# Gate terms on GpSimd, images' sum on VectorE, first gate at the head of the spectral part

## The chip, the cores and the metric

The kernel runs on one NeuronCore of a Trainium2 chip. The metric is the device time of one execution in microseconds; the time before is the median of three runs. The engines are called PE (TensorE), DVE (VectorE), ACT (ScalarE), POOL (GpSimd) and SP (SyncE, which here only issues DMAs).

## The reference

Two layers over x of shape 8x128x128x128 (images, channels, rows, columns), all in float32. Only the first layer is touched by the change. It computes, for each image:

```python
feat = gelu(batchnorm(conv2d(x, conv_w, padding=3, dilation=3)))      # 64 channels
F2 = fft2(feat)
attn = complex_softmax(einsum(l2norm(F2), conj(l2norm(F2))) * tau)    # within heads of 8 channels
out_f = abs(ifft2(attn @ F2))                                         # the mixture
cg = sigmoid(conv1x1(gelu(batchnorm(conv1x1(F2.real)))))              # the gate: 64 -> 4 -> 64
gate = abs(ifft2(cg * F2))                                            # the gated images
x = concatenate([out_f, gate], axis=1) + x
```

The second layer is a 3x3 convolution, a selective scan over eight tokens of every pixel, and a group norm, and takes the larger part of the time.

## The kernel before

`network` runs `layer0` and then `layer1`, with the result of the first in device memory (`x1`). `layer0` makes four passes over two images each; the two images' 64 channels fill the 128 partitions. A pass is `convolve` (the convolution, its transposes and the Gram matrix, 32 steps of four rows) and then `spectral`.

`spectral` works on groups of four channels of one image: 16 groups per image, n = 0 to 31 (`NP = 32`). The order of all engines' work is the order in which the program is written (`manual_schedule`): there is no planner, and every engine takes its own instructions strictly in that order. In iteration n of the loop (L444) stand, in this order:

- `columns(n)` (L288): the column transform on PE, into the PSUM banks `er` and `ei`.
- `gate_begin(n + 2)` (L310): the gate's base, four ACT instructions of 128x65 from the hidden map `hid`.
- `gated(n)` (L329): four DVE products of `er` or `ei` (PSUM) with the gate `cg` (SBUF), into `gp`.
- `rows(n + 1)` (L280): the row transform on PE, copied by ACT to `fa`.
- `rows_back(n - 1)` (L348): the last inverse transform on PE into `ops`; ACT takes the absolute value (L354), POOL adds the input images `xg` (L355), SP stores (L356).
- `gate_end(n + 2)` (L319): the gate's three remaining terms. Each is a product (L323) into the scratch tile `cgt` and an addition (L326) to `cg`, 128x260 elements; then ACT's sigmoid (L327), with a table load if ACT last used another set.
- `mixture()` (L377): from n = 3 on, once in an odd iteration and twice in an even one, four rows of the attention's output: PE into `pf` (one buffer of two banks), ACT's squares (L385, L386), DVE's sum (L387). For n of 1 and 2 the steps of `softmax` stand here instead.
- `columns_back(n)` (L340): PE into `zps`, and DVE's copy to `z` (L346).
- `roots()` (L394): after every fourth mixture, ACT's square root over 128x2048 (L397, with its own table load), POOL's addition of the input (L398, 128x2048), SP's stores and the loads for the next. Eight times in a pass.
- `load_gate(n + 3)` (L359): SP loads `xg`, into the buffer that the sum of group n releases in the next iteration.

After n = 24 there are no mixtures left. Every PSUM tile of `spectral` has one buffer: `ps`, `er`, `ei`, `zps`, `ops` and `pf` (two banks), beside `gram`. In SBUF `cg` and `xg` have three buffers, `cgt`, `fa`, `z`, `og` and `sq` two, `gp` one.

Ahead of the loop (L431 to L443) stand the hidden map of each of the two images (`rows` and `columns` of `mT`, then four Gelu instructions each), the first step of `softmax`, `rows(0)`, and both steps of the gate for groups 0 and 1.

The heart of what the change touches:

```python
for m in range(1, MID):
    t = f2.tile([P, 4, NF], F32, name="cgt")
    nc.vector.tensor_mul(t, hid[...].broadcast_to([P, 4, NF]), w2r[...].broadcast_to([P, 4, NF]))
    nc.vector.tensor_add(cgs[n], cgs[n], t)
nc.scalar.activation(cgs[n], cgs[n], AF.Sigmoid)
```

Of the kernel before, what the change touches and what calls it, by code (L numbers as in the profile page):

```python
# [10 lines left out]
AF = mybir.ActivationFunctionType  # L11
# [130 lines left out]
def layer0(ctx, tc, x, w0, c0, x1):  # L142
# [9 lines left out]
    nc = tc.nc  # L152
# [9 lines left out]
    def cf(name):  # L162
        at, n = C0[name]
        return ct[:, at:at + n]
# [32 lines left out]
    fT = big.tile([P, H, P], F32, name="fT")  # L197
# [68 lines left out]
    def spectral(p):  # L266

        with tc.tile_pool(name="l0_f1", bufs=1) as f1, \
# [9 lines left out]
            fas, cgs, zs, xgs, mix = {}, {}, {}, {}, {}  # L278

            def rows(key, src, j0):  # L280

                ps = p1.tile([P, 4, P], F32, name="ps")
                for k in range(4):
                    nc.tensor.matmul(ps[:, k], src[:, :, j0 + k], cf("fwd"), start=True, stop=True)
                fas[key] = f2.tile([P, 4, P], F32, name="fa")
                nc.scalar.copy(fas[key], ps)

            def columns(key, which):  # L288

                a, out = fas.pop(key), []  # L290
                for name, of_re, of_im in (("er", "cos", "sin"), ("ei", "nsin", "cos"))[:which]:
                    e = p1.tile([P, 4, NF], F32, name=name)
                    nc.tensor.matmul(
                        e, cf(of_re), a[:, :, 0:NF], start=True, stop=False, skip_group_check=True)
                    nc.tensor.matmul(
                        e[:, :, mid], cf(of_im), a[:, :, NF:P], start=False, stop=True,
                        skip_group_check=True)
                    out.append(e)
                return out

            def hidden(b):
                er, = columns(("m", b), 1)
                for m in range(MID):
                    nc.scalar.activation(
                        hid[:, b, m, :], er[:, m, :], AF.Gelu, bias=gt[:, m:m + 1], scale=gs[:, m:m + 1])

            def place(n):
                return n * 4 // CD, n * 4 % CD

            def gate_begin(n):  # L310
                b, c = place(n)
                cgs[n] = f3.tile([P, 4, NF], F32, name="cg")
                for i in range(4):
                    k = (c + i) * MID
                    nc.scalar.activation(
                        cgs[n][:, i, :], hid[:, b, 0, :], AF.Identity, bias=b2[:, c + i:c + i + 1],
                        scale=w2[:, k:k + 1])

            def gate_end(n):  # L319
                b, c = place(n)  # L320
                for m in range(1, MID):
                    t = f2.tile([P, 4, NF], F32, name="cgt")
                    nc.vector.tensor_mul(  # L323
                        t, hid[:, b, m:m + 1, :].broadcast_to([P, 4, NF]),
                        w2r[:, c:c + 4, m:m + 1].broadcast_to([P, 4, NF]))
                    nc.vector.tensor_add(cgs[n], cgs[n], t)  # L326
                nc.scalar.activation(cgs[n], cgs[n], AF.Sigmoid)  # L327

            def gated(n, e):  # L329
# [18 lines left out]
            def rows_back(n):  # L348
                (b, c), z = place(n), zs.pop(n)
                ops = p1.tile([P, 4, W], F32, name="ops")  # L350
                for i in range(4):
                    nc.tensor.matmul(ops[:, i, :], z[:, i, :], cf("inv"), start=True, stop=True)
                og, xg = f2.tile([P, 4, W], F32, name="og"), xgs.pop(n)
                nc.scalar.activation(og, ops, AF.Abs)  # L354
                nc.gpsimd.tensor_add(og, og, xg)  # L355
                nc.sync.dma_start(  # L356
                    x1[2 * p + b][CD + c:CD + c + 4, :, :].rearrange("c h w -> h c w"), og)

# [10 lines left out]
            def load_mixture(r0):  # L369
                mix[r0] = f2.tile([P, CH, W], F32, name="xr")  # L370
                for b in range(2):
                    nc.sync.dma_start(
                        mix[r0][b * CD:(b + 1) * CD], x[2 * p + b, 0:CD, r0:r0 + CH, :])
# [31 lines left out]
            def softmax(k):  # L405
                if k == 0:
                    nc.vector.tensor_copy(gm, gram)
                    nc.vector.tensor_mul(dg, gm, cf("ident"))
                    nc.vector.tensor_reduce(rn, dg, AX.X, ALU.add)
                    nc.vector.tensor_scalar(rn, rn, float(HW), NRM_EPS, ALU.mult, ALU.add)  # L410
                    nc.scalar.activation(rn, rn, AF.Sqrt)
                    nc.vector.reciprocal(rn, rn)
                    nc.vector.tensor_scalar(gm, gm, rn, None, ALU.mult)
                elif k == 1:
                    t = p1.tile([P, 2, 4, W], F32, name="pf")
                    nc.tensor.transpose(t[:, 0, 0, :], gm, cf("ident"))
                    nc.vector.tensor_scalar(gm, t[:, 0, 0, :], rn, tau_hw, ALU.mult, ALU.mult)
                    nc.vector.tensor_mul(gm, gm, cf("mask"))
                    nc.vector.tensor_add(gm, gm, cf("nmask"))
                    nc.vector.tensor_reduce(mx, gm, AX.X, ALU.max)  # L420
                    nc.vector.tensor_scalar(gm, gm, mx, None, ALU.subtract)
                    nc.scalar.activation(gm, gm, AF.Exp)
                elif k == 2:
                    nc.vector.tensor_reduce(rn, gm, AX.X, ALU.add)
                    nc.vector.reciprocal(rn, rn)
                    nc.vector.tensor_scalar(gm, gm, rn, None, ALU.mult)
                    t = p1.tile([P, 2, 4, W], F32, name="pf")
                    nc.tensor.transpose(t[:, 0, 0, :], gm, cf("ident"))
                    nc.vector.tensor_copy(pT, t[:, 0, 0, :])
# [3 lines left out]
            rows(("m", 0), mT, 0)  # L433
            hidden(0)
            rows(("m", 1), mT, MID)
            softmax(0)
            hidden(1)
            rows(0, fT, 0)
            load_mixture(H - CH)
            load_mixture(H - 2 * CH)  # L440
            for n in range(2):
                gate_begin(n)
                gate_end(n)  # L443
            for n in range(NP + 1):  # L444
                if n < NP:
                    e = columns(n, 2)
                    if n + 2 < NP:
                        gate_begin(n + 2)
                    gp = gated(n, e)
                    if n + 1 < NP:  # L450
                        b, c = place(n + 1)
                        rows(n + 1, fT, b * CD + c)
                if n > 0:
                    rows_back(n - 1)
                if n == NP:
                    break
                if n + 2 < NP:
                    gate_end(n + 2)
                if n >= START:
                    mixture()  # L460
                elif n > 0:
                    softmax(n)
                columns_back(n, gp)
                if n >= START and n % 2 == 0:
                    mixture()
                roots()
                load_gate(n + 3)
                if n == NP - 5 and 2 * p + 2 < B:
                    first_load(p + 1)
# [5 lines left out]
    with tc.manual_schedule(engines={E.PE, E.Activation, E.DVE, E.Pool, E.SP}):  # L475
        first_load(0)
        for p in range(B // 2):
            convolve(p)
            spectral(p)
# [593 lines left out]
```

## Time and profile before

| What | Value |
|---|---|
| Median of three runs | 15525.09 us (15520.91 to 15526.82) |
| The profiled execution: its time, its span | 15543.48 us, 15541.7 us |
| Granted clock of PE, mean | 0.98 |
| PE busy | 14740.9 us, 95% |
| DVE busy | 12858.9 us, 83% |
| POOL busy | 12025.9 us, 77% |
| ACT busy | 8249.8 us, 53% |
| POOL's sum of the images (L355), 128 times | 175.3 us, 1370 ns each |
| First layer ends in the profile at | about 2673 us |
| A pass's gate loop, from the first to the last z copy (first pass) | 358.4 to 675.8 us |

The page divides the span in 40 equal slices and gives the busy share of each engine in tenths. Its groups are instructions of one line, engine and shape: busy time and mean duration, then the engine's idle time before them and what ended most of it. The timeline gives start, duration, engine, line, and in brackets how long the engine was idle before and what released it. A table by stages gives each engine's busy time with the number of its instructions, the granted clock, the DMA share and the traffic.

### The profile page before, as it was taken

What the parts mean: (1) busy time and instruction counts of PE and PEld (TensorE: products, weight loads), DVE (VectorE), ACT (ScalarE), POOL (GpSimd) and SP (SyncE); (2) the same over time, 40 slices, a digit from 0 to 9 for tenths busy, and PEclk for the clock granted to TensorE, in tenths of its full rate; (3) what the DMA queues carried; (4) which work ended last, traced back from release to release, by engine and by line L of the source; (5) the groups of instructions that cost most, each with busy time, mean ns of one, the idle gap of its engine ahead of it and who ended that gap; (6) DMA issues with size and microseconds to landing.
All of it is one profiled execution on the core that took longest, in us unless ns stands there. A gap on an engine that the chain in (4) does not pass through costs nothing.

```text
span 15541.7 us, 200536 instructions
## 1 busy us (share of the span) xinstructions
PE 14740.9 (95%) x71816; PEld 5749.3 (37%) x71816; DVE 12858.9 (83%) x12667; ACT 8249.8 (53%) x9158; POOL 12025.9 (77%) x5796
## 2 busy tenths in 40 slices
PE   9899898999999999999999999999999999999996
PEld 4655556333333333333333333333333333333332
DVE  1423415999999999999999999999999999999995
ACT  1322314555555555555555555555555555555553
POOL 0101102899999999999999999999999999999996
PEclk9999999999999999999999999999999999999996
DMA  1323323666666666666666666666666666666665
GB/s 72 104 70 97 79 77 93 116 120 120 120 129 135 134 135 132 136 136 133 134 135 135 134 134 137 135 135 132 135 135 136 135 134 136 134 133 134 136 136 136
DMA packets 1075747, 1932.47 MB, mean 124 GB/s; under 512 B 123968, under 2 KB 255040, under 8 KB 1058368
## 3 DMA queue, kind: packets, MB, share of 16 engines
q1 hardware_dynamic: 1074176, 1917.29, 57.4%
q8 instruction: 571, 9.36, 0.2%
q14 instruction: 424, 3.47, 0.1%
q10 hardware_dynamic: 576, 2.35, 0.0%
HBM read 375.64 MB, written 201.33 MB: 37 GB/s over the span
## 4 chain that ended last, share of the span: by engine, by line
PE 58%; DVE 17%; issue 4%; ACT 3%; DMA 1%; POOL 0%; DVEq 0%; SPq 0%; POOLq 0%; ACTq 0%
PE da L693 18%; PE yps L759 8%; PE ups L693 7%; PE pm L134 7%; DVE da L724 6%; DVE h L732 4%; DVE h L708 4%; PE yps L765 4%; PE pm L645 3%; PE pm L778 3%; PE pm L657 3%; DVE hc L743 2%; PE da L638 2%; PE yps L749 2%; ACT da L698 2%
## 5 line engine op out<-in xcount | busy, mean ns | idle before, releaser
L738 POOL TENSOR_TENSOR hc<-h,cc 128x1024 f32<-128x1024 f32 x3584 | 8375.2, 2367 | 431.4 <-DVE h L732 409.1
L698 ACT ACTIVATE da<-da 128x1024 f32<-128x1024 f32 x3584 | 3618.7, 1010 | 4198.5 <-PE ups L693 2508.0
L708 DVE TENSOR_TENSOR h<-ups,bb 128x1024 f32<-128x1024 f32 x3584 | 4368.7, 1219 | 693.0 <-PE ups L693 313.5
L693 PE MATMUL da<-du,m_a 16*128 16x512 f32 x14336 | 4072.8, 644 | 139.3 <-DVE hc L743 135.2
L693 PE MATMUL ups<-du,m_u 16*128 16x512 f32 x14336 | 4119.2, 643 | 2.3 <-DVE h L708 1.3
L732 DVE TENSOR_TENSOR h<-da,h 128x1024 f32<-128x1024 f32 x2304 | 2821.2, 1224 | 79.1
L724 DVE TENSOR_TENSOR da<-da,h 128x1024 f32<-128x1024 f32 x2304 | 2820.1, 1224 | 6.9 <-ACT da L698 3.4
L134 PE MATMUL pm<-xin,l_wt 128*128 128x508 f32 (+1 forms) x4608 | 2413.0, 624 | 176.8 <-ACT xr L783 170.2
L730 POOL TENSOR_TENSOR h<-ah,h 128x1024 f32<-128x1024 f32 x768 | 1817.9, 2367 | 448.2 <-DVE ah L722 408.6
L693 PEld LDWEIGHTS da<-du,m_a 16*128 16x128 f32 x14336 | 1079.9, 184 | 2625.7 <-issue 1004.6
L759 PE MATMUL yps<-hc,l_ct 128*32 128x512 f32 x14336 | 1931.7, 611 | 0.0
L355 POOL TENSOR_TENSOR og<-og,xg 128x512 f32<-128x512 f32 x128 | 175.3, 1370 | 2126.3 <-ACT og L354 1065.7
L134 PEld LDWEIGHTS pm<-xin,l_wt 128*128 128x128 f32 x4608 | 751.7, 189 | 1620.6 <-issue 1390.6
L693 PEld LDWEIGHTS ups<-du,m_u 16*128 16x128 f32 x14336 | 1125.5, 184 | 379.4 <-DVE h L708 296.9
L241 DVE COPY fT<-tps 128x512 f32<-128x512 f32 x128 | 88.6, 692 | 1184.3 <-PE tps L240 1184.3
L698 ACT ACT_TABLE_LOAD x774 | 993.0, 1283 | 30.6 <-PE ups L693 1.7
L722 DVE TENSOR_TENSOR ah<-da,h 128x1024 f32<-128x1024 f32 x768 | 932.9, 1215 | 0.0
L134 PE MATMUL cps<-xin,l_wt 128*64 128x500 f32 (+1 forms) x4032 | 869.0, 584 | 0.0
L759 PEld LDWEIGHTS yps<-hc,l_ct 128*32 128x32 f32 x14336 | 283.8, 108 | 1376.7 <-issue 964.1
L652 POOL TENSOR_TENSOR u<-dt,xc 128x512 f32<-128x512 f32 x512 | 655.1, 1279 | 173.0 <-ACT dt L647 170.9
L235 ACT ACTIVATE feat<-cps,bn_t,bn_s 128x512 f32<-128x512 f32 x128 | 99.5, 777 | 1144.1 <-PE cps L134 1144.1
L647 ACT ACT_TABLE_LOAD x511 | 655.6, 1283 | 28.9 <-PE pm L645 1.1
(155 smaller groups left out, 15471.0 us busy)
## 6 DMA issues: line engine op xcount, KB each, us to landing
bb<-bc SPq DMA_DIRECT2D x2048, 256.0 KB
cc<-bc SPq DMA_DIRECT2D x2048, 256.0 KB
du<-dt SPq DMA_DIRECT2D x2048, 64.0 KB
du<-u SPq DMA_DIRECT2D x2048, 64.0 KB
xin<-x SPq DMA_DIRECT2D x112, 640.0 KB
xin<-x SPq DMA_DIRECT2D x48, 1408.0 KB
gn<-xr SPq DMA_DIRECT2D x256, 256.0 KB
v<-gn SPq DMA_DIRECT2D x256, 256.0 KB
```

The source lines that it names most:

```text
L134: nc.tensor.matmul(out[:, a:b, wa:wb], wt[:, t, :], src[:, r + dy + a - base:r + dy + b - base, wa + dx:wb + dx], start=(n == 0), stop=(n ...
L647: nc.scalar.activation(d["dt", hf], ps, AF.Softplus, bias=wf("dt_b"))
L652: nc.gpsimd.tensor_mul(d["u", hf], d["dt", hf], d["xc"][:, hf, :])
L693: nc.tensor.matmul(o, w, v, start=True, stop=True)
L698: nc.scalar.activation(da, da, AF.Exp)
L708: nc.vector.tensor_mul(h, d["ups", s], state_row(i, "bb", s // GP))
L722: nc.vector.tensor_mul(d["ah"], da, before)
L724: nc.vector.tensor_mul(da, da, before)
L730: nc.gpsimd.tensor_add(h, d["ah"], h)
L732: nc.vector.tensor_add(h, d["da", s], h)
L738: nc.gpsimd.tensor_mul(hc, d["h", s], state_row(i, "cc", t))
L759: nc.tensor.matmul(d["yps"][g * DI:(g + 1) * DI], gather[:, t % LP, :], d["hc", GP * t + g // GP][:, g % GP], start=False, stop=(t in (3, ...
```

## The change

Three edits, all in `spectral`:

1. `gate_end`: the three products and three additions are issued on GpSimd for n of 2 and up, and stay on VectorE for n of 0 and 1.
2. `rows_back`: ACT writes the absolute value back into PSUM (`ops`), and VectorE adds the input from there, in place of GpSimd.
3. The head: `gate_begin(0)` and `rows(0)` move ahead of `hidden(1)`, `gate_end(0)` ahead of `softmax(0)`; the loads of the mixtures and the gate of group 1 follow.

```diff
             def gate_end(n):
                 b, c = place(n)
+                eng = nc.vector if n < 2 else nc.gpsimd
                 for m in range(1, MID):
                     t = f2.tile([P, 4, NF], F32, name="cgt")
-                    nc.vector.tensor_mul(
+                    eng.tensor_mul(
                         t, hid[:, b, m:m + 1, :].broadcast_to([P, 4, NF]),
                         w2r[:, c:c + 4, m:m + 1].broadcast_to([P, 4, NF]))
-                    nc.vector.tensor_add(cgs[n], cgs[n], t)
+                    eng.tensor_add(cgs[n], cgs[n], t)
                 nc.scalar.activation(cgs[n], cgs[n], AF.Sigmoid)
...
                 og, xg = f2.tile([P, 4, W], F32, name="og"), xgs.pop(n)
-                nc.scalar.activation(og, ops, AF.Abs)
-                nc.gpsimd.tensor_add(og, og, xg)
+                nc.scalar.activation(ops, ops, AF.Abs)
+                nc.vector.tensor_add(og, ops, xg)
...
             rows(("m", 1), mT, MID)
+            gate_begin(0)
+            rows(0, fT, 0)
+            hidden(1)
+            gate_end(0)
             softmax(0)
-            hidden(1)
-            rows(0, fT, 0)
             load_mixture(H - CH)
             load_mixture(H - 2 * CH)
-            for n in range(2):
-                gate_begin(n)
-                gate_end(n)
+            gate_begin(1)
+            gate_end(1)
```

In the changed kernel two lines are added above these, so that L319 to L357 of before stand up to two lines later (the sigmoid at L329, the absolute value at L356, the sum at L357, POOL's large addition at L400).

## The prediction

> **What bounds the kernel now.** I read the page first: its slices of busy tenths say where the stages lie.
>
> ```profile
> span 15541.7 us, 200536 instructions
> ...
> DVE  1423415999999999999999999999999999999995
> ...
> POOL 0101102899999999999999999999999999999996
> ```
>
> A slice is 388.5 us. DVE and GpSimd are idle or light for some seven slices: that is the first layer, which ends at 2673 us in the timeline. The rest is the second layer, which the change doesn't touch. Within the first layer only the spectral part of each of the four passes changes. In the first pass it runs from 333 to 680 us, so four times about 345 us, 9% of the span, can move. The busy time by stage of that part:
>
> ```profile
> core 0: us, PE busy (x) PEld busy (x) DVE busy (x) ACT busy (x) POOL busy (x), PEclk, DMA share, GB/s
> 384.50:622.50 238.00, 192.53 (x927) 150.63 (x926) 144.75 (x252) 121.89 (x223) 59.67 (x27) 0.90 0.42 103
> 622.50:679.80 57.30, 53.07 (x331) 49.35 (x331) 38.21 (x79) 24.40 (x49) 16.17 (x10) 0.94 0.43 129
> ```
>
> While mixtures are interleaved (iterations 3 to 24, first row) PE is busy for 192.5 of 238 us; in the last iterations (second row) for 53.1 of 57.3. Near the end consecutive z copies stand at 659.02 and 665.09: 6.07 us per iteration, PE's own work. So the loop is PE's except where PE waits. The timeline shows where: after each of the eight `roots` of a pass. Iteration 9 of the first pass:
>
> ```profile
> 443.80 4.52 POOL L398 TENSOR_TENSOR feat<-feat,xr 128x2048 f32<-128x2048 f32 x1 [8.24 <-ACT feat L397]
> ...
> 445.08 3.53 DVE L326 TENSOR_TENSOR cg<-cg,cgt 128x260 f32<-128x260 f32 x1 [2.20 <-ACT cg L315]
> ...
> 448.28 1.46 POOL L355 TENSOR_TENSOR og<-og,xg 128x512 f32<-128x512 f32 x1
> ...
> 448.54 1.50 DVE L323 TENSOR_TENSOR cgt<-hid,l_wt 128x260 f32<-128x260 f32 x1
> ...
> 451.38 1.28 ACT L327 ACT_TABLE_LOAD   x1 [5.36 <-DVE cg L326]
> 452.67 0.42 ACT L327 ACTIVATE cg<-cg 128x260 f32<-128x260 f32 x1
> 453.00 0.58 ACT L385 ACTIVATE sq<-pf 128x512 f32<-128x512 f32 x1
> 453.61 0.58 ACT L386 ACTIVATE pf<-pf 128x512 f32<-128x512 f32 x1
> ...
> 454.22 0.69 DVE L387 TENSOR_TENSOR feat<-pf,sq 128x512 f32<-128x512 f32 x1 [2.92 <-ACT pf L386]
> 454.83 0.68 DVE L346 COPY z<-zps 128x512 f32<-128x512 f32 x1
> ...
> 455.66 2.05 PE L352 MATMUL ops<-l_ct,z 128*128 128x128 f32 x8 [5.25 <-ACT cg L315]
> ```
>
> Read it downwards. GpSimd's large add runs 443.80 to 448.32. The gate's add on DVE (0.43 us elsewhere) takes 3.53, the next product 1.50 (0.42 elsewhere) beside the images' sum. Then the sigmoid's table load, the sigmoid, the two squares queued behind it on ACT, their sum and the z copy on DVE, and at last PE, idle for 5.25 us and then at half clock (2.05 against 1.06). The gate's terms are what ends last there.
>
> **What the Trainium skill says.** "SBUF — State Buffer", Who interferes with whom: a VectorE instruction with two SBUF inputs blocks against a GpSimd one that reads SBUF; with one SBUF input, outside the 2-port modes, it doesn't. The trace agrees: 3.53 and 1.50 above, while the second layer's L708 (PSUM and SBUF) holds a mean of 1219 ns with GpSimd busy. "GPSIMD Engine Reference", Performance versus the Vector engine: about 2.6 cycles an element for two inputs, 4497 ns at 2048; the trace has 4.52 us. Same page, Performance pitfalls for Q7 kernels: reads with a step over 8 bytes cost about 50% more per element; no row here shows that. "ScalarE: Activation LUTs", What ACT_TABLE_LOAD costs: about 1283 ns; the trace has 1283.
>
> **Part 1: the gate's six terms (three products, three adds) go to GpSimd for n of 2 and up.** No row shows a 128x260 on GpSimd. Two rows of the page price it:
>
> ```profile
> L738 POOL TENSOR_TENSOR hc<-h,cc 128x1024 f32<-128x1024 f32 x3584 | 8375.2, 2367 | 431.4 <-DVE h L732 409.1
> ...
> L652 POOL TENSOR_TENSOR u<-dt,xc 128x512 f32<-128x512 f32 x512 | 655.1, 1279 | 173.0 <-ACT dt L647 170.9
> ```
>
> (2367-1279)/512 = 2.125 ns an element, 191 ns fixed, so 260 elements take 0.743 us (the line gives 4.54 at 2048; 4.52 is there). An add must wait for its product: I add 0.07, as from ACT's L354 end to GpSimd's L355 start in the first pass. A product needn't wait, and starts 0.04 before the last one's end (448.28 against 448.32). Six terms: 3x0.813 + 3x0.703 = 4.55 us; from the end of the gate's base on, 3.8, since the first product runs ahead.
> *Ordinary iterations.* In iteration 8 the base ends at 430.05, so the sigmoid starts at 433.9 against 434.34 now. The squares behind it wait for PE's mixture until 435.24 either way: nothing gained. ACT's loop, base 1.35 + 3.87 + sigmoid 0.33 = 5.55 us, stays under PE's 6.07.
> *Root iterations, seven per pass.* GpSimd now does the root's add and then all six terms, as the first product is queued behind the add too: 448.28 + 4.55 = 452.83, sigmoid at 452.90. The reload isn't late any more: in the built order of the changed program it waits only for ACT's own base and the sigmoid alone waits for GpSimd, whereas before the load waited for DVE. So 1.28 us of load is hidden, and the sigmoid comes at 452.90 against 452.67: +0.2 each, +1.4 per pass. The stall that the lock caused goes, and GpSimd's own queue takes its place.
> *The eighth root (n = 24)* has no squares behind it. There DVE's blocked terms hold the z copy until 640.22, PE stands 2.57 us and runs at half clock afterwards; the columns of n = 27 start at 646.30. After the change z is free at once; what is late next is ACT's fa copy, behind the sigmoid: GpSimd 637.3 + 4.55 = 641.9, sigmoid, base and fa to 644.2, and the columns then: -2.1, and half a step more without the half clock: -2.3 per pass.
>
> **Part 2: the images' sum goes to DVE, from PSUM.** `og<-ops,xg` has the form of L387, 0.69 us against 1.27 to 1.46 on GpSimd; ACT's L354 only changes where it writes, 0.60 as now. DVE gives up 6x0.43 and takes 0.69; with 61% busy in the first row above that is hidden. DVE now waits for og's store (ACT did), with the z copy queued behind it: before, this wait shows three times in all four passes, 3.4 us together, near a pass's end, and PE's work hid it: nothing. SP's loads wait for DVE in place of GpSimd, at the same places. The bank of `ops` is released by DVE and no longer by ACT, and the next pass's convolution waits for it (PE at 678.55, right after L354): +0.07 + 0.69, three times: +2.3 in all. No DVE instruction in the loop has two SBUF inputs any more outside softmax, so the lock has nothing to hold.
>
> **Part 3: the head.** Now the gated products start at 353.08. In the new order: base(0) at 339.99 to 341.43; its terms on DVE to 343.5; hidden(1) ends at 344.2 without its own reload (1.28 before); sigmoid(0) with load to 345.9; root load and rn to 347.4; base(1) to 348.9; its terms to 350.9; gated then: -2.2. Loads in the chain: three before, three after. In iteration 2 the softmax no longer follows the gate's terms on DVE (now 372.04): after L354 at 370.5 and the sum to 371.15 the three steps end at 371.95, PE at 372.05 against 372.88: -0.8.
>
> **Sum.** Per pass -2.2 - 0.8 + 1.4 - 2.3 = -3.9, four passes -15.6; + 2.3 at the seams; -0.6 for the last sum: -14 us. The profiled execution took 15543.48 us (span 15541.7 and 1.8 around), 18.4 over the median of 15525.09; I take the change from the median: 15511 us, -0.09%.
>
> **Bounds of the unknown price.** Below: nothing excludes a cheaper term; at -10% (0.67) the seven roots give 7x0.44 = 3.1 per pass more, and if the shorter idle of PE in the head (4.5 against 6.3 us) leaves the clock up, 1.6 more: -33 us, 15492. Above: the products read a weight that steps by 16 bytes; at +50% they take 1.11 and the mean term 0.93: roots 7x1.1 more, the ACT loop (rival a) at 6.5 against 6.07 in ten iterations 4.3, the mixtures' iterations some 4: 16, less 3.9: +12 per pass, 15575.
>
> **Rivals.** (a) *Slower: ACT's loop through GpSimd becomes the bound.* Every iteration passes base, terms, sigmoid on ACT in order. With terms of 1.0 us it takes 1.35 + 5.2 + 0.33 = 6.9, over 6.07; it decides from 0.84 on (5 terms fill 4.3). Ten iterations x 0.8, roots 7x1.7, mixtures some 8: +28, less 5 for the rest: +23 per pass, 15619. For it: an unmeasured broadcast form. Against it: L738 too has a broadcast operand and costs what the line says. (b) *Faster by more: the cheap end above,* 15492: the lock cost more than I see, in the ordinary iterations too (1.37 for the last add in many). Against it: PE or the root's queue ends last there. (c) *The load isn't hidden:* 1.28x7x4 = +36, 15547; against it stands the built order.
>
> **Chances.** Forecast with its neighbours, between 15494 and 15556: 0.63, with (c) in it at 0.05; (a) beyond that 0.20; (b) 0.17. A change under 0.2% (31 us) is about what a measurement of this kernel can't tell from none. The range takes the forecast's cases, most of (b) and the near half of (a): 15482 to 15575.
>
> **What would show it.** GpSimd 128x260 rows near 0.74 us; DVE's gate rows only for n of 0 and 1; no DVE row of 3.5; the sigmoid in root iterations 4.6 us after the root's add, its load long before; gated 2.2 us earlier in the head; the loop's last 6.07 unchanged. Terms over 0.84 us, or a load behind GpSimd's wait, would make me wrong.

## The result and the profile after

The changed kernel takes 15496.45 us (median of 20 runs, 15484.40 to 15508.01), the kernel before 15526.95 us (median of 20, 15520.91 to 15538.69): a ratio of 0.998, 95% interval 0.9973 to 0.9987. That is 30.5 us or 0.20% less, just at the border of what the prediction called no change; the interval lies wholly below 1. The forecast was 15511 us, 14 us less than before.

The page of the changed kernel, its span and the slices of VectorE and GpSimd:

```profile
span 15495.1 us, 200595 instructions
...
DVE  1211213999999999999999999999999999999995
...
POOL 0321304899999999999999999999999999999996
```

In the first layer's slices work has moved from VectorE to GpSimd; the rest reads as before. The table by stages of the first pass, over the same two stretches of the loop as before (from z copy 3 to z copy 23, and from there to the end of the pass):

```profile
379.80:612.30 232.50, 191.09 (x926) 149.90 (x926) 73.85 (x151) 122.15 (x224) 110.90 (x127) 0.90 0.42 105
612.30:667.60 55.30, 51.34 (x329) 47.52 (x329) 24.91 (x52) 25.12 (x51) 27.78 (x36) 0.99 0.45 138
```

VectorE's busy time in the first stretch falls from 144.8 to 73.9 us, GpSimd's rises from 59.7 to 110.9. The stretch itself gets only 5.5 us shorter, and PE's work and its granted clock (0.90) stay: 71 us of relief on an engine that had slack buy little.

The root iteration that the prediction took apart, in the timeline (start, duration, engine, line, work; in brackets the idle time before and what ended it):

```profile
439.23 4.52 POOL L400 TENSOR_TENSOR feat<-feat,xr 128x2048 f32<-128x2048 f32 x1 [9.76 <-ACT feat L399]
...
441.45 1.28 ACT L329 ACT_TABLE_LOAD   x1
...
443.71 0.63 POOL L325 TENSOR_TENSOR cgt<-hid,l_wt 128x260 f32<-128x260 f32 x1
444.41 0.74 POOL L328 TENSOR_TENSOR cg<-cg,cgt 128x260 f32<-128x260 f32 x1
...
447.21 0.73 POOL L328 TENSOR_TENSOR cg<-cg,cgt 128x260 f32<-128x260 f32 x1
...
447.98 0.42 ACT L329 ACTIVATE cg<-cg 128x260 f32<-128x260 f32 x1 [5.25 <-POOL cg L328]
...
450.14 0.68 DVE L348 COPY z<-zps 128x512 f32<-128x512 f32 x1
...
450.87 1.01 PE L354 MATMUL ops<-l_ct,z 128*128 128x128 f32 x3 [5.04 <-DVE z L348]
```

The table load now stands at 441.45, long before it is needed. The six terms follow GpSimd's large sum and take from 443.71 to 447.94. The sigmoid starts 8.75 us after that sum starts, where before it was 8.87 (452.67 - 443.80). PE idles 5.04 us instead of 5.25. So the stall is the same length, made of other parts.

GpSimd's new groups (busy time, mean ns of one, idle time before):

```profile
L328 POOL TENSOR_TENSOR cg<-cg,cgt 128x260 f32<-128x260 f32 x360 | 264.9, 736 | 357.1 <-issue 321.5 <-ACT cg L315 14.2
...
L325 POOL TENSOR_TENSOR cgt<-hid,l_wt 128x260 f32<-128x260 f32 x360 | 226.6, 630 | 1403.5 <-DVE cg L328 1403.5
```

The sum costs what the prediction's line gave (736 ns against 743), the product less (630 ns).

**Where the time went, per pass.** The z copies of the trace, one an iteration, give every part. The table has means of the four passes, before in us, the others as differences from it. Ordinary and root iterations are those between z copies 3 and 24: seven in which the sigmoid waits behind a square root, fourteen others. The seam runs from a pass's last z copy to the next pass's first Gelu (the fourth to the second layer's first matmul into `da`). The numbers in brackets are those of the experiments below. The median difference is each kernel's to the kernel before in the same comparison.

| Kernel | Convolution | Head | First three | Ordinary (14) | Roots (7) | Last seven | Seam | Sum x 4 | Median difference |
|---|---|---|---|---|---|---|---|---|---|
| before | 315.2 | 22.6 | 25.9 | 133.9 | 111.7 | 45.5 | 13.7 | | |
| after | +1.0 | -2.0 | -1.4 | -5.0 | -0.6 | -2.6 | +0.9 | -38.6 | -30.5 |
| terms alone (5) | 0.0 | +0.3 | +6.0 | +52.3 | +11.4 | +6.2 | -0.1 | +304.0 | +316.0 |
| sum alone (6) | 0.0 | -0.1 | +5.6 | +13.0 | -3.8 | -1.5 | +0.4 | +53.9 | +73.3 |
| head alone (3) | -0.1 | -2.3 | -0.2 | +0.6 | -0.1 | -0.6 | -0.1 | -10.8 | -10.1 |
| sum behind the terms (1) | 0.0 | -0.1 | -1.7 | -3.1 | -7.1 | -2.7 | +1.5 | -53.0 | -42.0 |
| after, bank by ACT (2) | 0.0 | -1.9 | -1.6 | -5.0 | -0.6 | -2.5 | -0.1 | -47.0 | -41.0 |
| after, products twice (4) | +1.0 | -1.8 | +2.3 | +7.1 | +14.0 | +1.9 | +0.2 | +99.2 | +102.6 |
| sum behind, head, old seam (7) | 0.0 | -2.4 | -1.2 | -3.0 | -7.4 | -2.7 | -0.3 | -67.7 | -51.9 |
| the same as 7, root's sum deferred (8) | 0.0 | -2.1 | -1.2 | -3.0 | -7.4 | -2.7 | -0.3 | -66.9 | -52.8 |
| the same as 7, early load (9) | -0.1 | -2.3 | -1.2 | -6.7 | -16.6 | -2.7 | -0.3 | -119.1 | -102.3 |
| after, root's sum deferred (10) | +1.0 | -2.1 | -1.2 | -2.8 | -25.8 | -3.8 | -0.3 | -139.7 | -133.0 |
| after, root's sum on VectorE (11) | 0.0 | -1.3 | -1.2 | -3.3 | -12.9 | -4.1 | -0.2 | -91.8 | -75.9 |
| last add on GpSimd (12) | 0.0 | -1.9 | -1.9 | -12.0 | -33.2 | -4.5 | -0.3 | -215.0 | -204.6 |

The profiled execution of before lay 16.5 us above its median (15543.48 against 15526.95). The sums over the passes come out up to 19 us lower than the differences of medians, and cells below about 0.6 say nothing: the head alone, which doesn't touch the ordinary iterations, shows +0.6 there.

### The profile page after: what moved, and what is told of

Read it like the earlier page. It is cut to its first block, busy times and chain, and to the rows that moved or that the text cites. A ratio compares the mean times of both kernels' runs of the same rounds, so it can differ in the third digit from the quotient of the medians.

```text
span 15495.1 us, 200595 instructions
## 1 busy us (share of the span) xinstructions
PE 14718.2 (95%) x71816; PEld 5738.3 (37%) x71816; DVE 12489.5 (81%) x12075; ACT 8246.5 (53%) x9158; POOL 12327.9 (80%) x6388
## 4 chain that ended last, share of the span: by engine, by line
PE 58%; DVE 17%; issue 4%; ACT 3%; DMA 1%; POOL 0%; DVEq 0%; SPq 0%; POOLq 0%; ACTq 0%
PE da L696 18%; PE yps L762 8%; PE ups L696 7%; PE pm L134 7%; DVE da L727 6%; DVE h L735 4%; DVE h L711 4%; PE yps L768 4%; PE pm L648 3%; PE pm L781 3%; PE pm L660 3%; DVE hc L746 2%; PE da L641 2%; PE yps L752 2%; ACT da L701 2%
## 5 line engine op out<-in xcount | busy, mean ns | idle before, releaser
L325 POOL TENSOR_TENSOR cgt<-hid,l_wt 128x260 f32<-128x260 f32 x360 | 226.6, 630 | 1403.5 <-DVE cg L328 1403.5
```

## The experiments

Line numbers in the profile lines are each kernel's own. No experiment leaves out part of the computation.

**1. The images' sum behind the terms** (e3_sum_late). My theory after seeing the result: in the ordinary iterations the lock on the gate's last term (VectorE's term is stretched from 0.43 to 1.38 us while GpSimd's sum of the images runs beside it) was on the path, and its end is the gain; GpSimd is not needed for it. The rival: the gain comes of VectorE being rid of the terms. The edit, to the kernel before:

```diff
-                nc.scalar.activation(og, ops, AF.Abs)
-                nc.gpsimd.tensor_add(og, og, xg)
+                nc.scalar.activation(ops, ops, AF.Abs)
+                return ops
...
                 if n + 2 < NP:
                     gate_end(n + 2)
+                if n > 0:
+                    images_sum(n - 1, ops)      # nc.vector.tensor_add(og, ops, xg), then the store
```

> The kernel before with one edit: the images' sum goes from GpSimd to VectorE and is issued after the next gate's terms instead of ahead of them; the terms stay on VectorE and the head stays as it was. In the kernel before, the images' sum on GpSimd runs beside VectorE's last term of the gate in ordinary iterations, and that term then takes 1.38 us where it takes 0.43 alone; so this edit takes that slowing away and nothing else that the change has. Theory 1 (the ordinary iterations' gain of some 5 us a pass came from this slowing of the last term, which held the sigmoid): the first-to-last distance of the images in a pass falls by 5 to 13 us, the last terms take 0.43 us, and the time is 15475 to 15505. Theory 2 (the gain came from VectorE being free of the terms themselves, so that its later work starts earlier): the time is 15518 or more, since VectorE then has 0.7 us more a group.

Measured: 15484.43 us, ratio 0.9973 (0.9962 to 0.9984). The first-to-last distance of the z copies falls by 14.7 us a pass, a little more than expected, and not where I had put it: 7.1 of it are in the seven root iterations. One of them in this kernel's timeline:

```profile
441.01 4.52 POOL L402 TENSOR_TENSOR feat<-feat,xr 128x2048 f32<-128x2048 f32 x1 [32.69 <-ACT feat L401]
...
442.30 3.51 DVE L326 TENSOR_TENSOR cg<-cg,cgt 128x260 f32<-128x260 f32 x1 [2.21 <-ACT cg L315]
...
446.99 0.43 DVE L326 TENSOR_TENSOR cg<-cg,cgt 128x260 f32<-128x260 f32 x1
...
447.50 1.28 ACT L327 ACT_TABLE_LOAD   x1 [4.28 <-DVE cg L326]
448.79 0.42 ACT L327 ACTIVATE cg<-cg 128x260 f32<-128x260 f32 x1
```

The block of 3.51 us by the root's sum stays, the second one (1.50 us in the kernel before) is gone: the sigmoid comes 7.78 us after the root's sum starts, 8.87 before. Without one instruction moved to GpSimd this kernel is as fast as the changed one or faster (the intervals of the two ratios overlap). So theory 1 holds in part: with the lock of the images' sum gone the ordinary iterations gain 3.1 us a pass, but more comes in the root iterations. The second theory, which asked for 15518 or more, falls. The edit moves the sum to VectorE as well as behind the terms; the new order alone, with the sum left on GpSimd, was not run. What the place is worth on VectorE, experiment 6 shows.

**2. The bank of the last group** (e6_seam). The changed kernel; in a pass's last group ACT writes to SBUF again:

```diff
-                nc.scalar.activation(ops, ops, AF.Abs)
-                nc.vector.tensor_add(og, ops, xg)
+                if n == NP - 1:
+                    nc.scalar.activation(og, ops, AF.Abs)
+                    nc.vector.tensor_add(og, og, xg)
+                else:
+                    nc.scalar.activation(ops, ops, AF.Abs)
+                    nc.vector.tensor_add(og, ops, xg)
```

> The changed kernel with one edit: for the last group of a pass alone, ScalarE writes its absolute value to SBUF as in the kernel before, and VectorE adds from there, so that the PSUM bank that the next pass's convolution needs is given back by ScalarE and not by VectorE. Theory A (the changed kernel's seam is longer because the bank waits for VectorE's sum, and the second half-speed stretch of TensorE after the seam follows from that longer idle time): the time from a pass's last image to the next pass's first Gelu falls from 11.0 to 10.0-10.3 us, the convolution after it from 316.1 to 314.8 us, together some 2 us in each of three seams, so 6 to 7 us: 15488 to 15491. Theory B (the half-speed stretch comes of the pass's shorter end or by chance): the seam shortens by 0.7 us and the stretch stays: 15494.

Measured: 15485.41 us, ratio to before 0.9974 (0.9965 to 0.9983). The three seams are 9.9 us long (after: 11.0) and the convolutions behind them 314.8 us (after: 316.1), 2.4 us a seam, 7 in all, as theory A asked; the time is 3 us under its band. (The intervals of the two kernels' ratios overlap; it is the trace that parts them.) The stages of 24 us from the start of the second pass's convolution, first of the changed kernel, then of this one (the last numbers but two are PE's granted clock):

```profile
666.00:690.00 24.00, 23.46 (x118) 10.03 (x120) 1.13 (x2) 2.84 (x3) 0.00 (x0) 0.93 0.63 252
```

```profile
667.00:691.00 24.00, 23.27 (x128) 10.34 (x128) 1.38 (x2) 3.44 (x4) 0.00 (x0) 1.00 0.64 255
```

PE's clock is 0.93 in the one and 1.00 in the other: 118 matmuls against 128 in the same time. The lost clock is one stretch of 3.4 us with which the changed kernel's convolution begins, right behind the wait:

```profile
666.50:670.00 3.50, 3.46 (x18) 2.13 (x20) 0.00 (x0) 1.28 (x1) 0.00 (x0) 0.51 0.24 75
```

In this pair PE's longer wait (1.44 us against 0.73) and the stretch go together at all three seams: 0.7 us of wait and 1.7 for the stretch are the 2.4. The other kernels show that the wait alone doesn't decide it. The same 1.44 us stands at every seam of five kernels of the table (after, 1, 4, 6 and 10), fifteen seams, and the stretch follows at nine of them: at none of experiment 6, at one of experiment 10. Where the wait is 0.7 us (1.0 at one seam), in the other nine kernels, it follows nowhere. What else decides stays open.

**3. The head alone** (e4_head): the third hunk of the change, on the kernel before.

> The kernel before with part 3 alone: the first group's gate goes to the head of the pass, ahead of the features' rows and the softmax. The prediction's step gave the head 2.2 us a pass and the softmax's place in the loop 0.8. If the parts add up: first rows' copy to first image falls from 22.6 to 20.6 us, the loop by under 1 us, 8 to 11 us in all: 15516 to 15519. If the head's gain needs the other parts (the loop's first steps wait for something else when the sums stay on GpSimd): 15524 to 15527.

Measured: 15516.37 us, ratio 0.9994 (0.9985 to 1.0002), which doesn't part it from no change by itself. The trace does: -2.3 us in the head of each pass. The first three intervals move by -0.2. The 0.8 that my expectation added here doesn't belong to this edit: the prediction had it from the gate's terms leaving VectorE ahead of the softmax, and in this kernel they still stand there.

**4. Every product twice** (e7_twice). The changed kernel, `tensor_mul` on GpSimd issued twice into the same tile: 3 x 0.628 = 1.88 us more GpSimd work a group.

> The changed kernel with each product of a gate's term on GpSimd issued twice (same output), 1.9 us more GpSimd work a group. It prices the term's cost on the path, which the rival of a slower result rested on. If the prediction's reading holds (in an ordinary iteration the sigmoid waits for GpSimd with little slack, in a root iteration with none): seven root iterations +1.9 each, and ScalarE's cycle of about 6.1 us at the end of a pass lengthens to 6.7 in some ten iterations: 15 to 25 us a pass, 15560 to 15600. If GpSimd has slack outside the root iterations: 13 us a pass or less, 15550 or under. If every iteration of the thirty pays in full: 57 us a pass, about 15725.

Measured: 15629.08 us, ratio 1.0068 (1.0053 to 1.0084): 132.6 us above the changed kernel, 33 a pass. The roots pay 2.1 us each. The fourteen ordinary iterations pay 12.1 together, where I had expected little outside the last ones, and the first three and the last seven 3.7 and 4.5. So my first reading was too low by a third: GpSimd has little slack in the ordinary iterations too. It puts a price on the rival that ended slower: it reckoned 28 us a pass for terms of 1.0 us, 1.54 us a group more than forecast; at 33 for 1.88, 1.54 cost 27.

**5. and 6. The parts alone.** The terms on GpSimd with the images' sum still in GpSimd's queue ahead of them (e1_terms, the first hunk):

> Part 1 of the change alone: the terms on GpSimd, the images' sum still on GpSimd ahead of them, the old head. The terms queue behind the images' sum, which waits for ScalarE's absolute value of the group before. If that queue sets the sigmoid's time, as the prediction's reading of the two queues says: some 4 us in each of thirty iterations, 15850 to 15950. If only the slowing of VectorE's terms mattered: about as the changed kernel, 15490 to 15510.

Measured: 15841.62 us, ratio 1.0204 (1.0190 to 1.0218), 8 us under the first expectation's band. An ordinary iteration of it:

```profile
453.09 1.26 POOL L356 TENSOR_TENSOR og<-og,xg 128x512 f32<-128x512 f32 x1 [4.86 <-ACT og L355]
...
457.81 0.73 POOL L327 TENSOR_TENSOR cg<-cg,cgt 128x260 f32<-128x260 f32 x1
...
458.57 0.42 ACT L328 ACTIVATE cg<-cg 128x260 f32<-128x260 f32 x1 [5.55 <-POOL cg L327]
```

GpSimd waits 4.86 us for the absolute value, and all six terms behind it. The second hunk alone, the sum on VectorE ahead of terms that stay there (e2_sum):

> Part 2 of the change alone: the images' sum on VectorE in its old place, ahead of the next gate's terms, which stay on VectorE; the old head. The sum waits for ScalarE's absolute value of the group before, and now VectorE's terms queue behind it: in an ordinary iteration they can start at some 4.2 us after the image instead of 1.9, and six at 0.42 then end at 6.7, where the slowed last term of the kernel before ended at 5.4. If that queue holds the sigmoid: over 1 us in each of some twenty iterations, 80 to 130 us in all, 15600 to 15660. If the lock's absence outweighs it, as when the sum stands behind the terms: 15490 to 15520.

Measured: 15598.10 us, ratio 1.0048 (1.0035 to 1.0062), 2 us under the first expectation's band. The same queue, now on VectorE:

```profile
466.32 0.69 DVE L355 TENSOR_TENSOR og<-ops,xg 128x512 f32<-128x512 f32 x1 [1.46 <-ACT ops L354]
466.93 0.42 DVE L323 TENSOR_TENSOR cgt<-hid,l_wt 128x260 f32<-128x260 f32 x1
...
469.52 0.42 ACT L327 ACTIVATE cg<-cg 128x260 f32<-128x260 f32 x1 [3.22 <-DVE cg L326]
```

The terms could have run from about 464.8, where VectorE has its gated products behind it; they begin at 466.93. Alone the parts cost 316 and 73 us, together they gain: only then do the images' sum and the terms stand in different queues. Against experiment 1, whose sum is on VectorE too but behind the terms, the place alone makes 114 us (15598.10 against 15484.43).

**7. What builds on it: sum behind the terms, head, old seam** (e9_best: the kernel of experiment 1 with the change's head, and the last three groups of a pass summed on GpSimd as before).

> The kernel before with the terms left on VectorE, the images' sum on VectorE after the next gate's terms (as in the run with that edit alone), the head of the change, and the last three groups of a pass summed on GpSimd as before. If the parts add: 42 off for the sum behind the terms, 10 off for the head, and the seam's 2.3 us in each of three passes back: 15526 - 59 = 15467 (15460 to 15475). If the head and the sum's place share the same microseconds: 15475 to 15482.

Measured: 15473.74 us, ratio 0.9968 (0.9957 to 0.9979). Head -2.4, roots -7.4, seam -0.3 us per pass: in the trace each part shows at its own stage at about its own size. The time lies in the band in which the parts add, 1.3 us from the other one, so by itself it doesn't part the two.

**8. The same with the root's sum issued one iteration later** (e10_best_defer: `root_sums()` behind `images_sum`).

> The run with the terms on VectorE, the sum behind them, the head and the old seam, with the root's 4.5 us sum on GpSimd issued one iteration later as well. There the root's sum stretched one of VectorE's terms to 3.5 us; issued later it falls beside other VectorE work. If that stretch was what the root iterations end on: 3 us in each of seven a pass, some 84 us, 15380 to 15400. If the lock only moves on to the images' own steps on VectorE: 15455 to 15475.

Measured: 15472.81 us, ratio 0.9967 (0.9955 to 0.9980). The time is in the second expectation's band, for neither reason. In both this kernel and the one of experiment 7 the root's sum starts 6.67 us after z copy 8 and blocks the same term for 3.53 us. GpSimd had nothing else in its queue, so a later place in it changed nothing. A miss of mine: a place in a queue only delays what has something ahead of it.

**9. The table load early** (e13_early_load: experiment 7's kernel with a sigmoid of one column after the absolute value, only in iterations after a square root).

```diff
                     nc.scalar.activation(ops, ops, AF.Abs)
+                    if warm:                     # filled by roots()
+                        warm.clear()
+                        t = f2.tile([P, 1], F32, name="warm")
+                        nc.scalar.activation(t, cf("ident")[:, :1], AF.Sigmoid)
```

> The run with the terms on VectorE, the sum behind them, the head and the old seam, with one addition: in an iteration after a square root ScalarE does a sigmoid of one column right after the absolute value, so that the 1.28 us table load stands there and not between the last term and the sigmoid. It prices the load that the prediction held hidden in the changed kernel and bare in the kernel before. If the bare load is on the path of the seven root iterations: 1.28 x 7 x 4 = 36 us, 15474 - 36 = 15438 (15432 to 15446). If something else ends just behind it: 15455 to 15475.

Measured: 15422.44 us, ratio 0.9934 (0.9922 to 0.9946), 51 us below experiment 7. The root iteration:

```profile
438.89 1.28 ACT L358 ACT_TABLE_LOAD   x1
...
442.66 0.43 DVE L326 TENSOR_TENSOR cg<-cg,cgt 128x260 f32<-128x260 f32 x1
...
443.18 0.42 ACT L327 ACTIVATE cg<-cg 128x260 f32<-128x260 f32 x1 [2.79 <-DVE cg L326]
```

The load lies beside the blocked terms, and the sigmoid follows the last term by 0.09 us. The roots gain 9.2 us a pass more, 1.31 each, which is the load; another 3.7 come in the ordinary iterations, which I hadn't expected and can't explain.

**10. The root's sum behind the terms, on GpSimd** (e8_defer: the changed kernel, `roots()` only takes the square root, and `root_sums()` with the sum, its stores and loads stands after the next `gate_end`).

> The changed kernel with one edit: a root iteration's 4.5 us sum on GpSimd, with its store, is issued one iteration later, behind the next gate's terms, so that the terms don't queue behind it. The prediction held that in the changed kernel this queue (root's sum, then six terms) is what the seven root iterations end on. If that holds, each loses some 4 us less: intervals of 17.6 fall to some 13 to 14, about 28 us a pass, 15370 to 15400. If another wait stands just behind it (ScalarE's table load and square root, or the mixture's own cost), the intervals fall by 1 to 2 us: 15440 to 15480. If the deferred sum locks VectorE at a worse place: 15490 or more.

Measured: 15392.58 us, ratio 0.9915 (0.9901 to 0.9928), as the first expectation had it. In the timeline, the end of a root iteration:

```profile
437.46 0.73 POOL L328 TENSOR_TENSOR cg<-cg,cgt 128x260 f32<-128x260 f32 x1
438.15 4.54 POOL L408 TENSOR_TENSOR feat<-feat,xr 128x2048 f32<-128x2048 f32 x1
438.22 0.42 ACT L329 ACTIVATE cg<-cg 128x260 f32<-128x260 f32 x1 [1.44 <-POOL cg L328]
```

Here the queue has something in it, and the order counts: the roots fall by 25.8 us a pass against the kernel before, and by 3.6 each against the changed kernel. Against it stands the next iteration, whose terms wait for the 4.54 us: 8.7 us, where the changed kernel has 7.5.

**11. The root's sum on VectorE** (e12_root_dve: experiment 10 with `nc.vector` for that sum, and experiment 2's bank).

> The changed kernel with the root's sum moved from GpSimd to VectorE and issued behind the next images' sum, and with the pass's last bank given back by ScalarE. In the run with the root's sum deferred on GpSimd, the iteration after a root was 8.7 us where the changed kernel has 7.5, since the 4.5 us sum stood ahead of that iteration's terms. On VectorE the sum of 2048 elements should take some 2.3 us (0.69 us for 512 and 0.43 for 260 elements give 1.04 ns an element) in a stretch where VectorE has nothing to do. If so: 1.1 us in each of seven a pass and some 4 us of the seams, 15393 - 35 = 15358 (15345 to 15370). If GpSimd's terms and VectorE's sum slow each other so that the terms end 2 us later: 15410 to 15450.

Measured: 15448.86 us, ratio 0.9950 (0.9937 to 0.9962): the second expectation.

```profile
441.13 2.82 DVE L412 TENSOR_TENSOR feat<-feat,xr 128x2048 f32<-128x2048 f32 x1
...
441.76 2.68 POOL L325 TENSOR_TENSOR cgt<-hid,l_wt 128x260 f32<-128x260 f32 x1
...
445.28 0.42 ACT L329 ACTIVATE cg<-cg 128x260 f32<-128x260 f32 x1 [3.49 <-POOL cg L328]
```

Now VectorE blocks GpSimd: the product takes 2.68 us instead of 0.63, and the sigmoid starts 5.61 us after GpSimd's first addition of this gate (at 439.67), where it was 3.56 in experiment 10 (438.22 - 434.66). The Trainium skill, "SBUF — State Buffer", Who interferes with whom, says "Issue order, not op shape, decides who blocks." This case shows both directions: 3.53 us for VectorE's addition in the kernel before, 2.68 for GpSimd's product here.

**12. All that held** (e14_last_add: experiment 9's kernel; the gate's last sum alone on GpSimd, the root's sum behind it).

```diff
-                    nc.vector.tensor_add(cgs[n], cgs[n], t)
+                    eng = nc.gpsimd if n > 1 and m == MID - 1 else nc.vector
+                    eng.tensor_add(cgs[n], cgs[n], t)
```

> Built from what the runs before showed, with no part of the computation left out: five of a gate's six instructions on VectorE, only the last sum of a gate on GpSimd; behind it on GpSimd, one iteration late, the root's 4.5 us sum, which so can't start before the gate is done and meets no two-operand work of VectorE until the next gate; the images' sum on VectorE behind the terms; the head of the change; the early table load; the last three groups of a pass as in the kernel before. If the root iterations end on the gate's chain alone: sigmoid at some 6.9 us after the image where the kernel with the root's sum deferred has 7.6, and the iteration after a root back from 8.7 to 7.8: 1.5 to 2 us for each root, 7 a pass, so 15393 - 50 = 15343 (15330 to 15360). If the next gate's terms on VectorE are stretched by the tail of the root's sum: 15380 to 15420.

Measured: 15318.95 us (4 runs, 15311.89 to 15324.75), ratio 0.9868 (0.9852 to 0.9885), 24 us better than expected and faster than both kernels.

```profile
434.49 0.73 POOL L327 TENSOR_TENSOR cg<-cg,cgt 128x260 f32<-128x260 f32 x1 [12.05 <-DVE cgt L323]
...
435.18 4.54 POOL L422 TENSOR_TENSOR feat<-feat,xr 128x2048 f32<-128x2048 f32 x1
435.26 0.42 ACT L328 ACTIVATE cg<-cg 128x260 f32<-128x260 f32 x1
...
439.34 0.68 DVE L323 TENSOR_TENSOR cgt<-hid,l_wt 128x260 f32<-128x260 f32 x1
```

One small instruction holds the large one back until the gate is done. VectorE works from PSUM meanwhile, and the next gate's first product loses 0.26 us (0.68 against 0.42), all that is left of the lock. From z copy 3 to z copy 23 of the first pass, the row that stands at the top for the changed kernel, read from this kernel's table by stages:

```profile
380.10:574.40 194.30, 180.39 (x924) 142.84 (x924) 110.20 (x251) 123.18 (x230) 46.12 (x27) 0.98 0.51 126
```

194.3 us instead of 232.5, and PE's granted clock is 0.98 instead of 0.90. With the shorter stalls most of PE's time at half clock is gone (by the clock records 3 to 7 us a pass between z copies 3 and 24, where the changed kernel has 44.4): PE is busy for 180.4 us instead of 191.1 with about as many matmuls, so 10.7 of the 38 us are PE's own work done faster. That the shorter stalls are the cause is likely, not shown.

## Why the prediction came out as it did

The direction was right and the time fell inside the stated range, but the gain is over twice the forecast (30.5 us against 14): the step that gave the larger part of it, the ordinary iterations, stood at nothing. That the result isn't further from the forecast is in part luck: misses of the other sign, at the seams and at the end of the last pass, cost 5.8 us that the forecast didn't have.

- *The price of a term* (0.743 us by the line through two other shapes): right for the sum (0.736), too high for the product (0.630). Six terms in a row took 4.23 us (443.71 to 447.94), not 4.55. The mean term, 0.683, is near the cheap end that the prediction priced. That L738 "costs what the line says" was no support: the line was drawn through it.
- *Root iterations, +0.2 each*: right in mechanism and nearly in size. The sigmoid followed the root's sum after 8.75 us, not 452.90 - 443.80 = 9.10, and so each gained 0.1: the whole miss is the term's price. That one stall took another's place is shown by experiment 10: with the queue in the other order, 3.6 us go from each root. What the hidden load was worth is shown on its sibling (experiment 9): 1.31 a root. At that price a bare load would have made the changed kernel's seven roots slower than before; that variant was not run. Rival (c) itself is settled by the trace: the load stands at 441.45, 6.5 us ahead of the sigmoid.
- *Ordinary iterations, nothing gained*: this step failed. It took iteration 8, where the squares wait for PE's mixture, for all of them. In the trace of before, in the second pass, the squares follow the sigmoid without a gap in nine of fourteen ordinary iterations: there the gate ends last, not the mixture. In the changed kernel they do in four. The iteration that ends with z copy 13 of the first pass, in the kernel before:

```profile
495.54 1.40 POOL L355 TENSOR_TENSOR og<-og,xg 128x512 f32<-128x512 f32 x1 [10.18 <-ACT og L354]
495.85 1.38 DVE L326 TENSOR_TENSOR cg<-cg,cgt 128x260 f32<-128x260 f32 x1
497.32 0.42 ACT L327 ACTIVATE cg<-cg 128x260 f32<-128x260 f32 x1 [1.86 <-DVE cg L326]
497.65 0.58 ACT L385 ACTIVATE sq<-pf 128x512 f32<-128x512 f32 x1
```

The last term takes 1.38 us beside the images' sum where 0.43 is its own, and the sigmoid and the squares queue behind it. Experiment 1, in which this meeting is gone and the terms stay where they were, gets 3.1 us a pass in these iterations. The change got 5.0 there. The 1.9 between them is not settled. By the clock records PE runs at half clock for 44.4 us between z copies 3 and 24 of a pass in the changed kernel and for 47.8 in experiment 1; half of the difference, 1.7, would be about the size. Where it comes from is not shown, and cells of the table are uncertain by 0.6. The prediction had this mechanism as its rival (b) and gave it 0.17.
- *Eighth root, -2.3 per pass*: -2.6 over the last seven iterations. PE waits there for ACT's `fa` copy behind the sigmoid (1.69 us, until 633.95), as said, and the loop's last intervals stay at 6.1 us. But experiment 1 gets 2.7 there with the terms on VectorE, so the terms' move was not needed for it.
- *Head, -2.2 per pass*: -2.0 in the changed kernel, -2.3 alone. *Softmax, -0.8*: held, and is a little more. The softmax now follows the images' sum on VectorE; its last copy (`pT`) comes 5.5 us after z copy 1 of a pass, where it was 6.6, and the interval between z copies 1 and 2 falls from 9.3 to 8.2 us in the mean. With the head alone the copy stays at 6.6. Experiment 1, with a shorter last term ahead of the softmax, gets it to 6.2.
- *Part 2, images' sum hidden on VectorE*: right; 692 ns against the 0.69 reckoned, and of the VectorE terms that were stretched before (78 additions and 36 products of the first layer) four additions are left, 0.76 us each, in the heads beside GpSimd's first product. What the step did not say is how much hangs on the place: ahead of terms on VectorE the same sum costs 73 us.
- *Seam, +2.3 in all*: right in mechanism, too small. The seam and the convolution behind it grew by 2.3, 2.3 and 2.0 us, together 6.7. The wait is as reckoned; the rest is the unforeseen half-clock stretch of 3.4 us with which the convolution begins. Experiment 2 gets both back. The wait itself, in the timeline of the changed kernel:

```profile
665.13 0.58 ACT L356 ACTIVATE ops<-ops 128x512 f32<-128x512 f32 x1 [3.43 <-PE ops L354]
665.75 0.69 DVE L357 TENSOR_TENSOR og<-ops,xg 128x512 f32<-128x512 f32 x1 [1.86 <-ACT ops L356]
...
666.54 11.84 PE L134 MATMUL cps<-feat,l_wt 128*64 128x512 f32 x56 [1.44 <-issue]
```

PE starts 1.41 us after ACT did; in the kernel before it was 0.65 (677.90 to 678.55): the 0.76 that was reckoned.

- *Last sum, -0.6*: this step failed. The last images' sum ends 0.75 us earlier after the last z copy (3.24 us, before 3.99), but the second layer's first matmul comes 0.2 later and its first into `da` 0.8 later. In both kernels what ends last there is the load of the second layer's weights (`l_wt`), which ACT issues behind the last absolute value, and not the sum.

- *Rival (a), slower*: its slope is confirmed by experiment 4 and its point was near (15619 for terms of 1.0 us; experiment 4 measured 15629). The six took 0.68 us each on average here and count for 1.00 there ((2 x 0.628 + 0.734) / 2): that is the difference between 30 us gained and 103 lost.

With the measured terms put in, -2.0 head, -1.4 first three, -5.0 ordinary, -0.6 roots and -2.6 last seven make -11.6 a pass, -46 in four; +6.7 at the three seams and +0.8 at the end of the last pass leave -39 for the first layer in the profiled executions, and the second layer, which the change doesn't touch, shows another 7.5 less. That the medians say -30.5 is the 16.5 us by which the profiled execution of before lay over its median; in which of its stages those lie can't be read.

## What to carry to other kernels

Read for every iteration which of two late arrivals ends last, not for one: a block of 1 us counts where it holds the last arrival, and the gate was the last in nine of fourteen. Before moving work to another engine to escape a lock, try to reorder it: putting one sum a group behind the terms (on VectorE, from PSUM) gave as much as the change that moves 720 instructions to GpSimd (42 and 30 us, with intervals that overlap), and with the new head, an early table load and a large sum held behind a small dependent one it came to 205. When parts of a change share a queue, price them together, since each alone can lose where both together gain.

## What the runs showed of the hardware

- GpSimd's product of two broadcast operands, 128x260, took 0.63 us, the sum of two contiguous ones of the same shape 0.736: the broadcast form was the cheaper, though the weight that it reads steps by 16 bytes from channel to channel.
- A GpSimd term started 0.07 us after the one that it depends on ended (444.34 to 444.41), and an independent product 0.04 before the last one ended (447.90 against 447.94).
- The lock takes either side: VectorE's 2048-element sum, 2.82 us, of which some 0.66 passed beside GpSimd's term ahead of it, then held a GpSimd product for 2.68.
- VectorE instructions with one operand in PSUM kept their 0.69 and 0.42 us beside GpSimd's 4.54 us sum in the last kernel.
- PE began a convolution with 3.4 us at half clock after a wait of 1.44 us at nine of fifteen seams, and at none of 27 after a wait of 0.7 to 1.0 us.
